# A two-layer transformer on one core: order of the first loads, the two norms between the layers, and halves at the end

## The chip, the core and the metric

The kernel runs on one core of a Trainium2 chip. The metric is device time in microseconds for one execution. Engines are called by their names in the profile: PE is TensorE (matrix products), PEld its weight loads, DVE is VectorE, ACT is ScalarE, POOL is GpSimd, SP is SyncE, which here only issues DMAs. Each engine works through its own instructions in the order in which the finished program has them, and waits on semaphores for the results of others.

## What is computed

The input x is 8×256 tokens of 128 numbers. Two layers follow, each an attention and a mixture of 8 experts of which every token takes 2, with a residual sum after each part:

```python
x = x + L0_attn(layernorm(x), ...)    # latent q/kv projections, rope, causal softmax
x = x + L0_ffn(layernorm(x), ...)
x = x + L1_attn(layernorm(x), ...)    # linear attention in segments of 32 tokens
x = x + L1_ffn(layernorm(x), ...)     # relu experts, not weighted
# L0_ffn, f being its input:
out = 0.5 * gelu(f @ shared_W + shared_b)
for e in range(8):
    out = out + combine[:, e:e+1] * (gelu(f @ W1[e] + b1[e]) @ W2[e] + b2[e])
out = (out - mean) * rsqrt(var + 1e-5) * gamma + beta
# L1_attn begins, x being its input (already a layernorm's output):
xn = x * rsqrt(mean(x * x) + 1e-6) * norm_w
q, k, v = xn @ Wq.T, xn @ Wk.T, xn @ Wv.T
```

So three norms follow one another between layer 0's experts and layer 1's projections: the norm of the experts' sum with gamma and beta, the layernorm of the new x (called `xl` in the kernel), and the root-mean-square norm of `xl`, whose factor r is applied after the projections.

## The kernel before

The tokens lie in 4 blocks of 512 (`NBLK`), each of 4 tiles of 128 tokens (`NT`); a block's x stays on chip as a tile [128, 4, 128]. Layer 0's attention (`attention0`) runs over rows of heads, two rows a block. Then each block goes through a chain of small steps and through the experts:

- `route0`: layernorm of x into `hrows`, transposes (L292), gate logits, choice of two experts, `dispatch`, which works out a slot for each token and copy, and eight indirect DMAs on POOL (L412) that scatter the rows `hrows` to the slots `xg` in DRAM.
- `experts`: 15 slots of 128 rows a block. SP loads the rows `xr` and the weights (256 KB a load), PE transposes the rows (L465, copied to `xrT` by DVE at L466) and does the products L482 and L494 with ACT's activation L489 between them; DVE copies the result `ys` (L502), SP stores it to `yg` in DRAM.
- `chosen`: eight indirect DMAs on POOL (L538) gather each token's two results as `yt`.
- `into_layer1` = `combine0` and `before1`. `combine0` adds the weighted `yt` to `acc` (eight operations of 128x128, L874), normalises `acc` by `layernorm` (scaled at L276), multiplies by gamma and adds beta on POOL (L883, L884), and adds the result to x on DVE (L886). `before1` takes the layernorm of x as `xl` (L276), then the statistics of `xl` for the second norm, transposes `xl` (L292) and projects it (L915).
- `attention1`: scores L1059, the mask product `at` on DVE (L1064), L1077, L1096 and further products on PE, with `vm` (L1002, L1140), `rec`, `on`, `xo` on POOL and DVE.
- `route1`, then `experts` and `chosen` again, and `finish`, which adds the two `yt` to x (L1281) and stores x to the output.

Every norm uses `moments` (per tile one statistics operation L265 and one aggregate L266 on DVE) and `rsqrt`: POOL adds eps (L256) and raises to the power −0.5 (L257), with the exponent from the tile `mhalf`.

At the start PE multiplies `wqa` by `wqb` and `wkva` by `wkvb` (L206, L208, with copies `oT` L207 and `wqkv` L211 to L214 on DVE), so that layer 0 has one projection; DVE multiplies the stacked layer-1 weights `wqkvu` by the norm's weight `nw` (L243). The loads are issued in text order on two queues: SP takes x0 to x3 first and then the weights, ACT takes `consts`, the rows of biases, and `nw`.

What is emitted when is set by `Lines`: a clock `now` that `go` advances by given times beside the attention's steps, and two queues, "chain" and "experts". Each step of a chain is due `APART` = 1.0 after the one before, or after the number that it yields; lags `SENT`, `STORED`, `BACK` = 5, 1, 5 stand before the experts, the gathers and `into_layer1` or `finish`. `behind(engine)` fixes what is emitted in it after the last instruction emitted for that engine; the rest is placed by the scheduler of the build. The result is one fixed order for each engine.

Of the kernel before, what the change touches and what calls it, by code (L numbers as in the profile page):

```python
# [34 lines left out]
ALU = mybir.AluOpType  # L35
# [28 lines left out]
    "before": P, "ones": P, "cap": E * NT, "upto": E * E, "slot": SL, "index": E,  # L64
    "ret": 2 * NSEG, "rev": E, "causal": P, "causalT": P, "pick": G * VA,
}
CAT, _n = {}, 0
for _k, _w in CONSTS.items():
    CAT[_k] = (_n, _n + _w)
    _n += _w  # L70
NCONST = _n


@with_exitstack
def two_layers(
# [67 lines left out]

    x_in = x.rearrange("(b t p) d -> b p t d", t=NT, p=P)
    out_v = out.rearrange("(b t p) d -> b p t d", t=NT, p=P)
    xs = []
    for b in range(NBLK):
        xb = tl(cp, [P, NT, D], f"x{b}")
        nc.sync.dma_start(out=xb, in_=x_in[b])
        xs.append(xb)  # L150

    def load(ap, shape, tag, eng=None):
        t = tl(cp, shape, tag)
        (eng or nc.sync).dma_start(out=t, in_=ap)
        return t
# [1 line left out]
    def load_row(ap, n, tag):  # L157
        return load(ap.partition_broadcast(P), [P, n], tag, nc.scalar)

    cs = load(consts, [P, NCONST], "consts", nc.scalar)  # L160

    def const(name):
        return cs[:, CAT[name][0] : CAT[name][1]]

    wqa_s = load(wqa, [D, QL], "wqa")
    wkva_s = load(wkva, [D, KVL], "wkva")
    wqb_s = load(wqb, [QL, D], "wqb")
    wkvb_s = load(wkvb, [KVL, KVH * HD * 2], "wkvb")
    wout_s = load(wout, [P, D], "wout")
    bout_s = load_row(bout, D, "bout")  # L170
    gw0 = load(gate_w0, [P, E], "gw0")
    shw = load(shared_w, [P, D], "shw")
    shb = load_row(shared_b, D, "shb")
# [21 lines left out]
    causb, causTb = tl(cp, [P, G, P], "causb", BF), tl(cp, [P, G, P], "causTb", BF)  # L195
    nc.vector.tensor_copy(causb, const("causal").unsqueeze(1).to_broadcast([P, G, P]))
    nc.vector.tensor_copy(causTb, const("causalT").unsqueeze(1).to_broadcast([P, G, P]))
    mhalf = tl(cp, [P, NT], "mhalf")
    nc.gpsimd.memset(mhalf, -0.5)


# [38 lines left out]
        yg.append(tl(dram, [SL * P, D], f"yg{h}"))  # L240


    nc.vector.tensor_scalar_mul(wqkvu[:, 0 : 3 * D], wqkvu[:, 0 : 3 * D], nw)  # L243


    vas = [tl(cp, [P, NT, H * VA + 32 - VA], f"va{k}") for k in range(2)]
    for t in vas:
# [4 lines left out]
    def rsqrt(src, eps):  # L252

        n = src.shape[1]
        r = tl(sm, [P, NT], "rsqrt")[:, 0:n]
        nc.gpsimd.tensor_scalar(r, src, eps, None, ALU.add)  # L256
        nc.gpsimd.tensor_tensor(r, r, mhalf[:, 0:n], ALU.pow)  # L257
        return r

# [570 lines left out]
    def route0(x, half):  # L830
        later = []
        xn = layernorm(x, half.rows, later)
        yield
        later[0]()
        yield
        with behind(PE):
            xT = transposed(xn, "xTf", "vec")
        yield
        lg = small("lg")
        with behind(PE):  # L840
            nc.vector.tensor_copy(lg, logits(xT, gw0))
            psh = bank().rearrange("p (t o) -> p t o", t=NT)
            for t in range(NT):
                nc.tensor.matmul(
                    psh[:, t, :], lhsT=xT[:, t * P : (t + 1) * P], rhs=shw, start=True, stop=True
                )
        half.acc = acc = tl(wk, [P, NT, D], "acc", bufs=NBLK)
        nc.vector.tensor_tensor(acc, psh, per_tile(shb), ALU.add)
        hots = half.hots
        m1, m2 = top2(lg, hots)  # L850
        yield 2 * APART
        yield from dispatch(half, b1s0)
        tot = small("tot", (P, NT))
        nc.vector.tensor_tensor(tot, m1, m2, ALU.add)
        nc.vector.reciprocal(tot, tot)
        gates = tl(wk, [P, 2, NT, E], "gates")
        for k, m in enumerate((m1, m2)):
            g = half.gates[:, k, :]
            nc.vector.tensor_tensor(g, m, tot, ALU.mult)
            nc.vector.tensor_tensor(gates[:, k], hots[:, k], last(g, E), ALU.mult)  # L860
        nc.vector.tensor_tensor(gates[:, 0], gates[:, 0], gates[:, 1], ALU.add)
        nc.scalar.activation(acc, acc, AF.Gelu)
        yield
        with behind(PE):
            nc.vector.scalar_tensor_tensor(
                acc, acc, 0.5, gated_bias(gates[:, 0], b2s0), ALU.mult, ALU.add
            )

    def combine0(x, half, yt):
# [6 lines left out]
                        acc[:, t, :], ALU.mult, ALU.add,  # L876
                    )
        yield
        later = []
        layernorm(acc, acc, later)  # L880
        yield
        later[0]()
        nc.gpsimd.tensor_tensor(acc, acc, per_tile(gam), ALU.mult)  # L883
        nc.gpsimd.tensor_tensor(acc, acc, per_tile(bet), ALU.add)  # L884
        yield
        nc.vector.tensor_tensor(x, x, acc, ALU.add)  # L886


    class Linear:
# [1 line left out]

    def before1(o, x):

        later = []
        xl = o.xl = layernorm(x, tl(wk, [P, NT, D], "xl"), later)
        yield
        later[0]()
        mv = moments(xl)
        ms = small("ms", (P, NT))
        nc.vector.tensor_tensor(ms, mv[:, :, 0], mv[:, :, 0], ALU.mult)  # L900
        nc.vector.tensor_tensor(ms, ms, mv[:, :, 1], ALU.add)
        r = rsqrt(ms, 1e-6)
        yield
        with behind(PE):
            xlT = transposed(xl, "xlT", "act", bufs=1)
# [278 lines left out]
    def route1(x, half):  # L1184
        later = []
        xn = layernorm(x, half.rows, later)
        yield
        later[0]()
        yield
        with behind(PE):  # L1190
# [79 lines left out]

    def into_layer1(b, half):
        yield from combine0(xs[b], half, half.yt)
        o = Linear()
        o.va = vas[b % 2]
        yield from before1(o, xs[b])
        linear[b] = o

    def finish(b, half):
        with behind(DVE):
            for k in range(2):  # L1280
                nc.vector.tensor_tensor(xs[b], xs[b], half.yt[:, k], ALU.add)  # L1281
        nc.sync.dma_start(out=out_v[b], in_=xs[b])
        yield

    def routed(b, layer):
# [119 lines left out]
```

## Time and profile before

| | us |
|---|---|
| median of 3 runs | 741.91 |
| the runs | 741.91, 733.67, 745.56 |
| profiled execution, its time | 770.52 |
| its span, first to last instruction | 768.8 |
| PE busy | 597.3 |
| PE idle, summed over its timeline | 154 up to its last product at 749.5 |
| mean granted clock of PE | 0.897 of full speed |

All lines of the profile are from the one profiled execution. A line of a timeline gives the start, the duration, the engine, the source line, the operation with output and inputs and the shape, and in brackets how long the engine stood idle before it and which instruction ended that wait. The chain of waits is followed back from the last instruction of the program. Between 0 and 20 us PE is busy 4.54 us: the first loads, `x0` at 6.1 and `wqa` at 10.84, come in; `nw` lands at 13.42 and `wvt`, part of `wqkvu`, at 15.55. PE's last product ends at 749.5; after it come the store of `yg`, the eight last gathers (752.93 to 762.6), the sums and the store of the output.

### The profile page before, as it was taken

Reading aid. Unit: us, or ns where it says so; the run is one execution under the profiler, and the core shown is the slowest. Engines: PE = TensorE matmul, PEld = TensorE weight load, DVE = VectorE, ACT = ScalarE, POOL = GpSimd, SP = SyncE. Lnnn points to the kernel's source line nnn. Section 1 sums busy time; section 2 is a strip of 40 time slices with the busy share of each in tenths; the row PEclk is TensorE's granted clock in tenths of the full one; section 3 lists DMA queues with packets and bytes.
Section 4 is the critical chain, followed back from the end, with each engine's and each line's share of the span. In section 5 each row is a group of like instructions: output and inputs, shape, how many; then the busy total and the mean of one; then the engine's idle time right before and its main releaser. Section 6 shows DMA issues by size and latency. Waiting matters only on the chain.

```text
span 768.8 us, 13323 instructions
## 1 busy us (share of the span) xinstructions
PE 597.3 (78%) x4654; PEld 454.3 (59%) x4654; DVE 402.1 (52%) x1161; ACT 339.3 (44%) x765; POOL 208.3 (27%) x269
## 2 busy tenths in 40 slices
PE   2578785998787788859988678879887799696880
PEld 1233343676464565439677567658685778595770
DVE  3656574446445565256845584656664476461111
ACT  0243332878758599415732231643234333342440
POOL 5200114010441304322123324050613250512303
PEclk9999978899989799878989796997988899897996
DMA  6500004353535133325434344354443456686761
GB/s 182 170 1 1 1 1 146 112 151 111 165 91 163 41 104 114 103 76 148 132 117 127 103 121 123 115 155 124 138 140 121 148 156 198 182 240 181 219 207 52
DMA packets 131890, 95.70 MB, mean 124 GB/s; under 512 B 8736, under 2 KB 114288, under 8 KB 131824
## 3 DMA queue, kind: packets, MB, share of 16 engines
q1 hardware_dynamic: 126400, 85.32, 37.7%
q0 software_dynamic: 4096, 8.40, 3.6%
q10 hardware_dynamic: 1328, 1.15, 0.5%
q8 instruction: 37, 0.61, 0.3%
q14 instruction: 29, 0.24, 0.1%
HBM read 77.79 MB, written 17.04 MB: 123 GB/s over the span
## 4 chain that ended last, share of the span: by engine, by line
PE 49%; DVE 16%; issue 9%; ACT 9%; DMA 7%; POOL 7%; SPq 2%; another core or an unknown queue 1%; POOLq 0%; ACTq 0%; DVEq 0%
PE mm L482 11%; PE mm L494 10%; PE sc L758 5%; POOL yt L538 3%; ACT at L705 2%; DMA w<-in_w 2%; PE mm L1077 2%; PE sc L763 2%; PE mm L1096 2%; DVE at L1064 2%; PE sc L915 2%; PE sc L1059 2%; PE mm L716 2%; DVE nmax L666 2%; ACT L489 1%
## 5 line engine op out<-in xcount | busy, mean ns | idle before, releaser
L489 ACT ACTIVATE hT<-mm,bias 128x128 f32<-128x128 f32 x480 | 135.9, 371 | 165.7 <-PE mm L482 123.4
L482 PE MATMUL mm<-xrT,w 128*128 128x128 f32 x960 | 149.7, 308 | 25.9 <-issue 10.6
L482 PEld LDWEIGHTS mm<-xrT,w 128*128 128x128 f32 x960 | 135.9, 219 | 42.1 <-issue 18.7
L494 PE MATMUL mm<-w,hT 128*128 128x128 f32 x960 | 144.2, 293 | 15.2 <-ACT hT L489 11.5
L494 PEld LDWEIGHTS mm<-w,hT 128*128 128x128 f32 x960 | 130.1, 206 | 22.8 <-ACT hT L489 18.3
L412 POOL DMA_INDIRECT xg<-hrows,slots x64 | 66.5, 1038 | 125.3 <-DVE slots L405 95.3
L538 POOL DMA_INDIRECT yt<-yg,slots x64 | 61.1, 955 | 87.1 <-DMA yg<-ys 52.9
L705 ACT ACTIVATE at<-sc 128x1024 f32<-128x1024 f32 x48 | 48.8, 1022 | 55.9 <-PE sc L763 32.8
L758 PE MATMUL sc<-qm,kxT 32*128 32x512 f32 x192 | 53.6, 679 | 14.6 <-DVE nmax L666 6.8
L758 PE MATMUL sc<-km,qT 32*128 32x512 f32 x192 | 53.6, 680 | 3.9 <-DVE qx L666 2.0
L502 DVE COPY ys<-mm 128x512 f32<-128x512 f32 (+1 forms) x32 | 21.0, 655 | 63.2 <-PE mm L494 47.7
L666 DVE TENSOR_REDUCE nmax<-sc 128x8 f32<-128x1024 f32 x32 | 38.8, 1219 | 25.3 <-PE sc L763 12.7
L1064 DVE TENSOR_TENSOR at<-sc,consts 128x1024 f32<-128x1024 f32 x32 | 38.0, 1215 | 17.2 <-PE sc L1059 6.6
L489 ACT ACT_TABLE_LOAD x27 | 34.6, 1283 | 11.0 <-PE mm L482 10.6
L256 POOL TENSOR_SCALAR rsqrt<-mv 128x4 f32<-128x4 f32 (+1 forms) x24 | 5.9, 245 | 102.2 <-DVE mv L266 96.9
L466 DVE COPY xrT<-mm 128x512 f32<-128x512 f32 (+1 forms) x32 | 20.8, 650 | 21.6 <-PE mm L465 21.1
L758 PEld LDWEIGHTS sc<-qm,kxT 32*128 32x128 f32 x192 | 14.4, 193 | 28.5 <-issue 10.2
L1083 ACT COPY rope<-mm 128x512 f32<-128x512 f32 x16 | 9.4, 586 | 49.0 <-PE mm L1077 27.8
L716 PE MATMUL mm<-at,vx 128*32 128x512 f32 x192 | 27.2, 635 | 4.7 <-ACT at L705 3.9
L666 DVE TENSOR_REDUCE qx<-sc 128x8 f32<-128x1024 f32 x16 | 19.6, 1224 | 20.2 <-PE sc L763 18.0
L1059 PE MATMUL sc<-pqm,kT 32*128 32x512 f32 x128 | 20.0, 696 | 12.8 <-DVE at L1064 9.0
L763 PEld LDWEIGHTS <-identb 128*128 128x128 bf16 x128 | 10.0, 98 | 33.6 <-issue 26.3
(211 smaller groups left out, 988.1 us busy)
## 6 DMA issues: line engine op xcount, KB each, us to landing
w<-in_w SPq DMA_DIRECT2D x240, 256.0 KB
xr<-xg SPq DMA_DIRECT2D x24, 256.0 KB
yg<-ys SPq DMA_DIRECT2D x24, 256.0 KB
xg<-zero SPq DMA_DIRECT2D x12, 256.0 KB
xr<-xg SPq DMA_DIRECT2D x8, 192.0 KB
yg<-ys SPq DMA_DIRECT2D x8, 192.0 KB
x<-in_x SPq DMA_DIRECT2D x4, 256.0 KB
xg<-hrows,slots POOLq DMA_INDIRECT x64
```

Source lines behind the costliest of these rows:

```text
L412: i = nc.gpsimd.indirect_dma_start(out=xg_h[:, :], out_offset=bass.IndirectOffsetOnAxis(ap=half.slots[:, k, t : t + 1], axis=0), in_=half. ...
L482: nc.tensor.matmul(ph[:, c * P : (c + 1) * P], lhsT=w1s[:, c * P : (c + 1) * P], rhs=xrT[:, t * P : (t + 1) * P], start=True, stop=True,)
L489: nc.scalar.activation(hT[:, c, :], src, func, bias=bias)
L494: nc.tensor.matmul(po[:, t * D : (t + 1) * D], lhsT=hT[:, c, :], rhs=w2s[:, c, :], start=(c == 0), stop=(c == NC - 1),)
L538: nc.gpsimd.indirect_dma_start(out=yt[:, k, t, :], out_offset=None, in_=yg[half.h][:, :], in_offset=bass.IndirectOffsetOnAxis(ap=half.slot ...
L666: return nc.vector.tensor_reduce(nm[:, js[0] : js[0] + 2, :], sc.rearrange("p j (i k) -> p j i k", i=G), AX.X, ALU.max, negate=True,)
L705: return nc.scalar.activation(pT[:, js[0] : js[0] + 2, :], sc, AF.Exp)
L716: nc.tensor.matmul(self.po[32 * j : 32 * j + 32, :], lhsT=self.vx[:, kt, j, :], rhs=self.pT_of[s][:, j, :], start=(kt == 0), stop=(kt == qt),)
L758: nc.tensor.matmul(out_, lhsT=lhsT, rhs=rhs, start=True, stop=mask is None)
L763: done[n].append(nc.tensor.matmul(out_.rearrange("p (i k) -> p i k", i=G), lhsT=identb, rhs=mask, start=False, stop=True,))
L1059: nc.tensor.matmul(sc[j].rearrange("p (i k) -> p i k", i=G), lhsT=pkT[rows, cols], rhs=pqm[rows, :, cols], start=True, stop=True,)
L1064: nc.vector.tensor_tensor(at[:, 2 * a : 2 * a + 2].rearrange("p j i k -> p (j i) k"), d.rearrange("p j (i k) -> p (j i) k", i=G), const("t ...
```

## The change

The first loads are issued in another order: x0, `wqa` and `wkva` on SP, `wqb` and `wkvb` on ACT's queue, `consts` in two pieces (the first 646 columns, then 990), and x1 to x3 behind them. The product of `wqkvu` and `nw` moves in the text from the set-up to the first `into_layer1`. `rsqrt` adds eps on DVE. `route0` adds beta to x on POOL once the layernorm's rows are scaled; the sum after the experts then leaves it out. `combine0` scales with gamma in the same operation as the mean's subtraction, before the power is known, and applies the power in the sum with x. `before1` takes both norms from one set of statistics of x: with v the variance of x, the mean of `xl` squared is v/(v+1e-5), so one power of 2×4 columns gives both factors. Steps that wait for a power are due 1.5 `APART` later. `finish` adds and stores in two halves of two tiles.

```diff
@@ -64,11 +64,12 @@
     "before": P, "ones": P, "cap": E * NT, "upto": E * E, "slot": SL, "index": E,
     "ret": 2 * NSEG, "rev": E, "causal": P, "causalT": P, "pick": G * VA,
 }
+SOON = ("cos", "sin", "sub", "first")
 CAT, _n = {}, 0
 for _k, _w in CONSTS.items():
     CAT[_k] = (_n, _n + _w)
     _n += _w
-NCONST = _n
+NCONST, NSOON = _n, CAT[SOON[-1]][1]
 
 
 @with_exitstack
@@ -143,12 +144,6 @@
 
     x_in = x.rearrange("(b t p) d -> b p t d", t=NT, p=P)
     out_v = out.rearrange("(b t p) d -> b p t d", t=NT, p=P)
-    xs = []
-    for b in range(NBLK):
-        xb = tl(cp, [P, NT, D], f"x{b}")
-        nc.sync.dma_start(out=xb, in_=x_in[b])
-        xs.append(xb)
-
     def load(ap, shape, tag, eng=None):
         t = tl(cp, shape, tag)
         (eng or nc.sync).dma_start(out=t, in_=ap)
@@ -157,17 +152,22 @@
     def load_row(ap, n, tag):
         return load(ap.partition_broadcast(P), [P, n], tag, nc.scalar)
 
-    cs = load(consts, [P, NCONST], "consts", nc.scalar)
+
+    xs = [load(x_in[0], [P, NT, D], "x0")]
+    wqa_s = load(wqa, [D, QL], "wqa")
+    wkva_s = load(wkva, [D, KVL], "wkva")
+    wqb_s = load(wqb, [QL, D], "wqb", nc.scalar)
+    wkvb_s = load(wkvb, [KVL, KVH * HD * 2], "wkvb", nc.scalar)
+    cs = tl(cp, [P, NCONST], "consts")
+    for cols in (slice(0, NSOON), slice(NSOON, NCONST)):
+        nc.scalar.dma_start(out=cs[:, cols], in_=consts[:, cols])
 
     def const(name):
         return cs[:, CAT[name][0] : CAT[name][1]]
 
-    wqa_s = load(wqa, [D, QL], "wqa")
-    wkva_s = load(wkva, [D, KVL], "wkva")
-    wqb_s = load(wqb, [QL, D], "wqb")
-    wkvb_s = load(wkvb, [KVL, KVH * HD * 2], "wkvb")
+    bout_s = load_row(bout, D, "bout")
+    xs += [load(x_in[b], [P, NT, D], f"x{b}") for b in range(1, NBLK)]
     wout_s = load(wout, [P, D], "wout")
-    bout_s = load_row(bout, D, "bout")
     gw0 = load(gate_w0, [P, E], "gw0")
     shw = load(shared_w, [P, D], "shw")
     shb = load_row(shared_b, D, "shb")
@@ -195,7 +195,7 @@
     causb, causTb = tl(cp, [P, G, P], "causb", BF), tl(cp, [P, G, P], "causTb", BF)
     nc.vector.tensor_copy(causb, const("causal").unsqueeze(1).to_broadcast([P, G, P]))
     nc.vector.tensor_copy(causTb, const("causalT").unsqueeze(1).to_broadcast([P, G, P]))
-    mhalf = tl(cp, [P, NT], "mhalf")
+    mhalf = tl(cp, [P, 2 * NT], "mhalf")
     nc.gpsimd.memset(mhalf, -0.5)
 
 
@@ -240,8 +240,6 @@
         yg.append(tl(dram, [SL * P, D], f"yg{h}"))
 
 
-    nc.vector.tensor_scalar_mul(wqkvu[:, 0 : 3 * D], wqkvu[:, 0 : 3 * D], nw)
-
 
     vas = [tl(cp, [P, NT, H * VA + 32 - VA], f"va{k}") for k in range(2)]
     for t in vas:
@@ -253,7 +251,7 @@
 
         n = src.shape[1]
         r = tl(sm, [P, NT], "rsqrt")[:, 0:n]
-        nc.gpsimd.tensor_scalar(r, src, eps, None, ALU.add)
+        nc.vector.tensor_scalar(r, src, eps, None, ALU.add)
         nc.gpsimd.tensor_tensor(r, r, mhalf[:, 0:n], ALU.pow)
         return r
 
@@ -830,8 +828,9 @@
     def route0(x, half):
         later = []
         xn = layernorm(x, half.rows, later)
-        yield
+        yield 1.5 * APART
         later[0]()
+        nc.gpsimd.tensor_tensor(x, x, per_tile(bet), ALU.add)
         yield
         with behind(PE):
             xT = transposed(xn, "xTf", "vec")
@@ -876,14 +875,20 @@
                         acc[:, t, :], ALU.mult, ALU.add,
                     )
         yield
-        later = []
-        layernorm(acc, acc, later)
-        yield
-        later[0]()
-        nc.gpsimd.tensor_tensor(acc, acc, per_tile(gam), ALU.mult)
-        nc.gpsimd.tensor_tensor(acc, acc, per_tile(bet), ALU.add)
-        yield
-        nc.vector.tensor_tensor(x, x, acc, ALU.add)
+
+        with behind(DVE):
+            mv = moments(acc)
+            r = rsqrt(mv[:, :, 1], 1e-5)
+            for t in range(NT):
+                nc.vector.scalar_tensor_tensor(
+                    acc[:, t, :], acc[:, t, :], mv[:, t, 0:1], gam, ALU.subtract, ALU.mult
+                )
+        yield 1.5 * APART
+        with behind(DVE):
+            for t in range(NT):
+                nc.vector.scalar_tensor_tensor(
+                    x[:, t, :], acc[:, t, :], r[:, t : t + 1], x[:, t, :], ALU.mult, ALU.add
+                )
 
 
     class Linear:
@@ -891,15 +896,25 @@
 
     def before1(o, x):
 
-        later = []
-        xl = o.xl = layernorm(x, tl(wk, [P, NT, D], "xl"), later)
-        yield
-        later[0]()
-        mv = moments(xl)
-        ms = small("ms", (P, NT))
-        nc.vector.tensor_tensor(ms, mv[:, :, 0], mv[:, :, 0], ALU.mult)
-        nc.vector.tensor_tensor(ms, ms, mv[:, :, 1], ALU.add)
-        r = rsqrt(ms, 1e-6)
+
+        xl = o.xl = tl(wk, [P, NT, D], "xl")
+        with behind(DVE):
+            mv = moments(x)
+            v, rr = mv[:, :, 1], small("norms", (P, 2, NT))
+            nc.vector.tensor_scalar(rr[:, 0], v, 1e-5, None, ALU.add)
+            nc.vector.reciprocal(rr[:, 1], rr[:, 0])
+            nc.vector.tensor_tensor(rr[:, 1], rr[:, 1], v, ALU.mult)
+            nc.vector.tensor_scalar(rr[:, 1], rr[:, 1], 1e-6, None, ALU.add)
+            rr = rr.rearrange("p a t -> p (a t)")
+            nc.gpsimd.tensor_tensor(rr, rr, mhalf, ALU.pow)
+        r = rr[:, NT:]
+        yield 1.5 * APART
+        with behind(DVE):
+            for t in range(NT):
+                nc.vector.tensor_scalar(
+                    xl[:, t, :], x[:, t, :], mv[:, t, 0:1], rr[:, t : t + 1],
+                    ALU.subtract, ALU.mult,
+                )
         yield
         with behind(PE):
             xlT = transposed(xl, "xlT", "act", bufs=1)
@@ -1184,7 +1199,7 @@
     def route1(x, half):
         later = []
         xn = layernorm(x, half.rows, later)
-        yield
+        yield 1.5 * APART
         later[0]()
         yield
         with behind(PE):
@@ -1270,16 +1285,21 @@
 
     def into_layer1(b, half):
         yield from combine0(xs[b], half, half.yt)
+        if b == 0:
+
+            nc.vector.tensor_scalar_mul(wqkvu[:, 0 : 3 * D], wqkvu[:, 0 : 3 * D], nw)
         o = Linear()
         o.va = vas[b % 2]
         yield from before1(o, xs[b])
         linear[b] = o
 
     def finish(b, half):
-        with behind(DVE):
-            for k in range(2):
-                nc.vector.tensor_tensor(xs[b], xs[b], half.yt[:, k], ALU.add)
-        nc.sync.dma_start(out=out_v[b], in_=xs[b])
+        for t in range(0, NT, 2):
+            x = xs[b][:, t : t + 2]
+            with behind(DVE):
+                for k in range(2):
+                    nc.vector.tensor_tensor(x, x, half.yt[:, k, t : t + 2], ALU.add)
+            nc.sync.dma_start(out=out_v[b][:, t : t + 2], in_=x)
         yield
 
     def routed(b, layer):
```

## The prediction

> **What bounds the kernel now.** I read the page's busy shares first, then its chain of waits, then TensorE's timeline for gaps, and last VectorE's and GpSimd's timelines inside the largest gaps. The page:
>
> ```profile
> PE 597.3 (78%) x4654; PEld 454.3 (59%) x4654; DVE 402.1 (52%) x1161; ACT 339.3 (44%) x765; POOL 208.3 (27%) x269
> ...
> PE 49%; DVE 16%; issue 9%; ACT 9%; DMA 7%; POOL 7%; SPq 2%; another core or an unknown queue 1%; POOLq 0%; ACTq 0%; DVEq 0%
> ```
>
> TensorE is busy for 78% of the span and is half of the chain; VectorE and GpSimd together are 23% of it. What the change can win is therefore the time in which TensorE stands and waits for them. Adding up the holes of TensorE's timeline gives 154 us, most of it in holes under 1.5 us that no part of this change addresses; two large ones sit at the chain it rewrites.
>
> ```profile
> 254.92 1.15 PE L292 MATMUL mm<-ident,xl 128*128 128x128 f32 x4 [7.59 <-DVE xl L276]
> 339.49 2.09 PE L1059 MATMUL sc<-pqm,kT 32*128 32x512 f32 x8 [6.71 <-DVE at L1064]
> ```
>
> Columns: start, duration, what, and in brackets the idle time before it with its releaser. The first is block 0's way from layer 0 to layer 1, followed back in the chain of waits:
>
> ```profile
> 247.17 1.13 DVE acc L276 x4
> 248.37 1.27 POOL acc L883
> 249.71 1.27 POOL acc L884
> ...
> 253.36 1.04 POOL rsqrt L257
> 254.92 1.15 PE mm L292 x4
> ```
>
> It is a serial relay VectorE–GpSimd–VectorE–GpSimd–VectorE. The second gap is block 1, in VectorE's timeline:
>
> ```profile
> 333.68 1.12 DVE L276 TENSOR_SCALAR acc<-acc,mv,rsqrt 128x128 f32<-128x128 f32 x4 [1.09 <-POOL rsqrt L257]
> 334.71 1.22 DVE L1064 TENSOR_TENSOR at<-sc,consts 128x1024 f32<-128x1024 f32 x1
> 337.51 0.69 DVE L886 TENSOR_TENSOR x<-x,acc 128x512 f32<-128x512 f32 x1 [1.59 <-POOL acc L884]
> 338.12 1.22 DVE L1064 TENSOR_TENSOR at<-sc,consts 128x1024 f32<-128x1024 f32 x1
> ```
>
> TensorE needs the two mask products L1064 of attention 1; they stand in VectorE's order behind the norm of `acc` and the sum L886, which wait for GpSimd. What blocks is the place in the order, not the work.
>
> **What the Trainium skill says.** "GPSIMD Engine Reference", section 4.1 Engine selection: two-input elementwise work belongs on VectorE, about twice as fast there. The trace agrees: 128x512 takes 1.27 us on GpSimd (L883) and 0.69 on VectorE (L886). "SBUF — State Buffer", section Who interferes with whom: a VectorE instruction with two SBUF inputs is blocked while a GpSimd instruction reads SBUF. The trace shows what looks like it: the 128x32 product L317 takes 1.27 us at 446.93, while L883 runs on GpSimd from 446.89. "TensorE: Matmul & The Clock Gate", its table of clock states: an idle window of some 3.4 us ends in half rate. The granted clock agrees in direction: 0.74 in the window 240–260 and 0.75 in 325–350, against 0.897 over the span.
>
> **The sum, part by part**, against the profiled execution (770.52 us, span 768.8). That one is 3.9% above the median of the runs, 741.91; I carry the ratio over.
>
> *First loads.* TensorE starts at 10.84 when `wqa` lands, but its work stops again until `xn` at 16.70; `xn` (16.30) waits in VectorE's order behind L243, the `wqkvu` product, which waits for the DMA of `wvt` until 15.57. The text moves L243 to the first chain, but in the changed program's instruction order it is still VectorE's 24th instruction, now between the two copies of `oT` (L207). So it stays at the start and holds the second copy. Its inputs: `nw` landed at 13.42 behind 11 ACT issues, and now stands behind 14, each about 0.4; the three `wq/wk/wv` loads have three issues fewer ahead on SP (0.37–0.39 each). I put the product at about 13.7, then the second `oT` copy, its matmul (0.68), three `wqkv` copies (0.5), `xn` at 15.6: −0.7. Bounds: −3 (loads as early as `x0`, which landed at 6.1) and +1.5 (the ACT queue slips by three waits).
>
> *Block 0's chain.* Gone: L883 and L884 (2×1.27), one add L256 (0.25), L886 (0.69) against four products of 128x128 (4×0.27), eight statistics of `xl`. New: four small VectorE operations (about 0.1–0.2 each) and a power of 128x8. A power of 128x2 takes 0.70 and of 128x4 1.04, so 1.72 by the same slope. That alone would be −2.5. But VectorE's new order puts `nmax` L666 (1.19), `qx` and the copy `os` L722 (0.68) between the two norms, which ran in the shadow of GpSimd before. Step by step from 244.4: scaling and eps 0.9, power 1.04, the four sums 1.1, statistics 1.0, the inserted 2.0, small operations 0.9, power 1.7, `xl` 0.4: about 253.9 for L292. −1.0; bounds 0 and −3.
>
> *Block 1's chain.* In the new order two L1064, `os`, `rec`, `on`, another L1064 and L746 all stand ahead of the statistics of `acc`. The eight sums L874 end at 330.94; two L1064 (1.13 each) to 333.2, `os` 0.6, L730 1.0, `rec` and `on` 0.5, two L565 with L567 and L570 2.5: L465 comes at about 338.0 instead of 347.01. Four L1059 (1.05) are then still to do, so −8.0. Late next is `xl`; by the same step lengths it is ready near 346.5, before TensorE reaches its transposes (near 348), so nothing is given back there. Bounds: −4 (`xl` or `xrT` L466, now behind the norm, holds TensorE) and −11 (the clock of that window rises from 0.75 to 0.897: 15.8 us of matmul become 13.2).
>
> *Blocks 2 and 3.* Two gaps at 448.54 (2.30) and 456.74 (1.99) and a stall of 0.64 come from L1064 and `cap` L382 behind norm work and the 1.27 block of L317. I take 3 of the 4.9. In block 3 VectorE waits 1.58 and 1.36 for GpSimd, with a TensorE gap of 2.07: −2. Bounds for both together: 0 and −8.5.
>
> *Route 1 of block 2.* Its power waited behind eight final gathers of block 0 (588.74–598.6) and TensorE then stood 4.57. In the new GpSimd order it stands ahead of them. Half: −2.3; bounds 0 and −4.6.
>
> *End.* The last gather lands at 764.23; then two sums (0.69 each) and a store. By halves: two sums of 128x256 (0.42 each) before the first store, two hidden under it, a second store of half the size: −0.6; bounds 0 and −1.
>
> *At nothing.* The early addition of `beta` to `x` (a 128x512 sum on GpSimd, 1.27 by L884, four times) runs while VectorE and TensorE do the routing; without that cover it costs up to 1.27 each, +5 in all. The eps additions moved to VectorE: 0.1 each, 24 times before, beside its 48% idle. Four more store issues on SP, 0.39 each, queued ahead of weight loads: hidden by the buffers of the weights; 1.6 without.
>
> Sum: −0.7 −1.0 −8.0 −3.0 −2.0 −2.3 −0.6 = −17.6, 752.9 us in that execution, a ratio of 0.977, **725 us** on the median. With all bounds at their good end (−3, −3, −11, −8.5, −4.6, −1 = −31) it is 712; with all at their poor end (+1.5, 0, −4, and nothing else) 739.5, or 741.0 with the 1.6 of the stores.
>
> **Rivals.** (a) *The gaps only move*, chance 0.27: block 1 gains half (−4), blocks 2 and 3 nothing, because the weights' loads and ACT hold TensorE there anyway; −7, **735 us**. For it: the idle shares of TensorE in many small holes, and ACT named for hidden-layer waits (L494, 11.5 us idle). Against: both large gaps name VectorE. (b) *GpSimd's order turns against it*, chance 0.10, slower: in the new order block 0's eight final gathers stand directly ahead of the eight scatters of block 2's layer 1, 16×1.25 = 20 us in one piece, and the gathers wait for the store of `yg` (a wait of that kind shows 4.94 at 312.65). If slots are ready when the gathers start, scatters are late by up to 4.9+10+1.8 (`vm`) = 16.7, at two places 33.4; with −15.3 left of the rest, +18, **759 us**. It decides from about 8 us per place on. Against: at 624.02 the scatters waited 3.82 for their slots, 25 us after the gathers ended. (c) *The change does not do what it says*: the product L243 is not moved, by the instruction order. That costs at most the 1.5 above and is inside the forecast.
>
> **How the numbers follow.** Forecast 0.63, rival (a) 0.27, rival (b) 0.10. The likeliest case's own range is 712–740; 8 in 10 with the run-to-run spread of before (733.67–745.56) and half of (a)'s poor end gives 710–743. About 2% (15 us) is what can be told from no change: 727 and below is faster. The forecast at 725 is near that border; its cases below it and a part above, with the block-1 clock gain on the other side, make faster 0.60, within 2% 0.30, slower 0.10.
>
> **What would show it.** Right: L292 after `xl` of block 0 about 1 us earlier with `nmax` and `os` in between; no gap of over 3 us ahead of L1059 in block 1 and L465 some 9 us earlier; a granted clock above 0.75 in that stretch; `xl` of block 1 ready before TensorE; no GpSimd wait of over 1 us in VectorE's norm chain of blocks 2 and 3. Wrong: a new gap of 4 us or more before the `xl` transposes of block 1 or the `xrT` copy, scatters L412 waiting on gathers, or VectorE's 24th instruction later than 15 us.

## The result and the profile after

| | before | after |
|---|---|---|
| median, us | 742.88 (733.67 to 747.98, 20 runs) | 736.45 (729.05 to 738.7, 20 runs) |
| ratio | | 0.9939, 95% interval 0.9911 to 0.9966 |
| profiled execution, us | 770.52 | 737.91 |

The change gains 0.6%, some 4.5 us: about a quarter of the 17.6 that the sum gave, and the forecast of more than 2% was wrong. The ratio compares, of each kernel, only the runs within 1.5% of its fastest; the quotient of the two medians is 0.991, and in the sets below the two measures differ by up to 0.007, so that smaller differences between kernels are not shown. The two profiled executions can't be subtracted: the one before lies 28 us above its median, the one after lies near its own. The kernel before took a median of 742.9, 779.4, 772.7, 772.9, 741.4 and 778.1 us in the six sets of comparisons of this study; only ratios go across. For the stages I set the profile after beside one of the old order with a like median (741.4 us in its set): the kernel with only the end by halves, `halves_only` below, whose orders are the old ones but for the final sums and stores. Its span is 739.8 us, the changed kernel's 736.1.

The page of the changed kernel, busy shares and chain of waits:

```profile
PE 583.3 (79%) x4654; PEld 443.2 (60%) x4654; DVE 408.8 (56%) x1177; ACT 341.9 (46%) x767; POOL 197.6 (27%) x233
...
PE 3%; DMA 2%; POOL 2%; issue 2%; ACT 0%; DVE 0%; POOLq 0%; SPq 0%; ACTq 0%; DVEq 0%
```

This chain could be followed back only through the last part of the span (its shares add up to 9%), so it says nothing of the stages before; the gaps of TensorE's timeline have to be read instead. First the old order, TensorE's timeline of `halves_only`, of which only lines with a gap that is spoken of below are shown (start, duration, what, idle time before it and its releaser):

```profile
256.98 1.15 PE L292 MATMUL mm<-ident,xl 128*128 128x128 f32 x4 [7.59 <-DVE xl L276]
342.96 2.09 PE L1059 MATMUL sc<-pqm,kT 32*128 32x512 f32 x8 [14.10 <-DVE at L1064]
410.03 1.49 PE L1059 MATMUL sc<-pqm,kT 32*128 32x512 f32 x8 [2.20 <-DVE vm L1140]
423.64 1.24 PE L292 MATMUL mm<-ident,hrows 128*128 128x128 f32 x4 [5.67 <-DVE hrows L276]
427.27 2.07 PE L482 MATMUL mm<-xrT,w 128*128 128x128 f32 x8 [2.39 <-DVE xrT L466]
446.13 1.14 PE L1059 MATMUL sc<-pqm,kT 32*128 32x512 f32 x8 [2.31 <-DVE at L1064]
580.70 1.63 PE L494 MATMUL mm<-w,hT 128*128 128x128 f32 x8 [4.58 <-ACT hT L489]
678.61 1.09 PE L465 MATMUL mm<-ident,xr 128*128 128x128 f32 x4 [4.68 <-DMA xr<-xg]
```

And, picked in the same way, the changed kernel's (its L290, L728, L1074, L463 and L480 are L292, L730, L1059, L465 and L482 of before):

```profile
258.59 1.24 PE L290 MATMUL mm<-ident,xl 128*128 128x128 f32 x4 [5.94 <-DVE xl L914]
339.92 1.92 PE L728 MATMUL mm<-consts,os 128*128 128x36 f32 x8 [6.86 <-DVE os L720]
402.85 2.08 PE L480 MATMUL mm<-xrT,w 128*128 128x128 f32 x8 [4.14 <-DVE on L1120]
426.18 2.09 PE L1074 MATMUL sc<-pqm,kT 32*128 32x512 f32 x8 [11.01 <-DVE rsqrt L254]
672.15 1.12 PE L463 MATMUL mm<-ident,xr 128*128 128x128 f32 x4 [8.28 <-DMA xr<-xg]
690.86 2.08 PE L480 MATMUL mm<-xrT,w 128*128 128x128 f32 x8 [6.42 <-DMA w<-in_w]
```

The gaps that the forecast promised to shorten did get shorter: block 0 from 7.59 to 5.94, block 1 from 14.10 to 6.86, and those at 446 and 581 are gone. But there is a gap of 11.01 that no part of the sum contained, one of 4.14, and longer waits for the last block's rows and weights. Up to its last product TensorE stands idle for 142.4 us in the old order (721.6 less 579.2 busy) and 134.6 in the new (717.9 less 583.3): 7.8 us less, though the four gaps that got shorter give back 15.8. Its busy time is 4.1 us longer, so its last product ends only 3.7 us earlier. Why the same number of products took longer stays open; the products right after a long gap did take about twice as long here (L1074 2.09 us at 426.18, behind the 11.01, and 1.14 at 414.03).

What the gap of 11 us waits for stands in VectorE's timeline of the changed kernel:

```profile
415.22 0.28 DVE L263 BATCH_NORM_STATS2 bnst<-x 128x6 f32<-128x128 f32 x1
415.54 0.18 DVE L264 BATCH_NORM_AGGREGATE mv<-bnst 128x2 f32<-128x6 f32 x1
423.42 0.29 DVE L263 BATCH_NORM_STATS2 bnst<-x 128x6 f32<-128x128 f32 x1 [7.71 <-POOL x L1164]
423.63 1.21 DVE L1079 TENSOR_TENSOR at<-sc,consts 128x1024 f32<-128x1024 f32 x1
...
426.02 0.68 DVE L464 COPY xrT<-mm 128x512 f32<-128x512 f32 x1
```

and in GpSimd's:

```profile
413.16 0.99 POOL L536 DMA_INDIRECT yt<-yg,slots  x1 [7.55 <-issue]
...
421.96 0.94 POOL L536 DMA_INDIRECT yt<-yg,slots  x1 [0.30 <-issue]
422.93 0.46 POOL L1164 TENSOR_TENSOR x<-x,hr 128x128 f32<-128x128 f32 x1
```

Block 0's attention 1 ends with four sums of the retrieved part into x (L1164, on GpSimd, 0.46 us). The last of them stands behind the eight gathers of block 2's experts, 413.16 to 422.90. The statistics of route 1 wait for it, and the masks L1079 of block 1, which TensorE needs next, stand behind these statistics in VectorE's order; so does the copy `xrT` for the next experts' products.

VectorE's wait for this sum is not new. The old order has it too, 8.59 us in `halves_only`, and TensorE did not stand through it:

```profile
410.92 0.68 DVE L466 COPY xrT<-mm 128x512 f32<-128x512 f32 x1
420.19 0.29 DVE L265 BATCH_NORM_STATS2 bnst<-x 128x6 f32<-128x128 f32 x1 [8.59 <-POOL x L1149]
```

```profile
411.65 3.21 PE L482 MATMUL mm<-xrT,w 128*128 128x128 f32 x16
```

There the copy `xrT` stands ahead of the waiting statistics, so TensorE has experts' products from 411.65 to 417.98 and is left with gaps of 5.67 and 2.39. In the new order masks and copy both stand behind the wait, and TensorE has nothing to do. What the change made is this re-laying, not the wait: in five profiles of kernels that have the old order here (`before`, `before_again`, `loads_only`, `before_last`, `halves_only`) VectorE waits 7.68 to 8.59 us for the sum, in five with the new one (the changed kernel, `after_again`, `chain_only`, `all_held`, `all_last`) 7.68 to 7.71. The gap of 4.14 at 402.85 lies at another place of this kind, a sum L1164 behind the eight scatters L410, for which VectorE waits 5.69.

The start, VectorE of the changed kernel:

```profile
14.66 0.42 DVE L1290 TENSOR_SCALAR wqkvu<-wqkvu,nw 128x384 f32<-128x384 f32 x1 [3.54 <-DMA nw<-in_norm_w]
14.99 0.27 DVE L207 COPY oT<-mm 32x128 f32<-32x128 f32 x1
...
16.45 2.44 DVE L274 TENSOR_SCALAR xn<-x,mv,rsqrt 128x128 f32<-128x128 f32 x6
```

`wqa` now lands in time for TensorE to start at 4.12 instead of 10.84, but the product with `nw` waits until 14.66 and holds the second copy of `oT`; `xn` comes at 16.45, against 16.30 before.

### The profile page after: what moved, and what is told of

It reads as the page before. It is cut to its first block, busy times and chain, and to the rows that moved or that the text cites. A ratio compares the mean times of both kernels' runs of the same rounds, so it can differ in the third digit from the quotient of the medians.

```text
span 736.1 us, 13320 instructions
## 1 busy us (share of the span) xinstructions
PE 583.3 (79%) x4654; PEld 443.2 (60%) x4654; DVE 408.8 (56%) x1177; ACT 341.9 (46%) x767; POOL 197.6 (27%) x233
## 5 line engine op out<-in xcount | busy, mean ns | idle before, releaser
L480 PE MATMUL mm<-xrT,w 128*128 128x128 f32 x960 | 146.3, 303 | 22.3 <-DMA w<-in_w 10.0
L480 PEld LDWEIGHTS mm<-xrT,w 128*128 128x128 f32 x960 | 132.8, 215 | 38.2 <-DVE xrT L464 10.2
L492 PE MATMUL mm<-w,hT 128*128 128x128 f32 x960 | 139.5, 287 | 7.9 <-ACT hT L487 6.6
L492 PEld LDWEIGHTS mm<-w,hT 128*128 128x128 f32 x960 | 126.1, 201 | 15.4 <-ACT hT L487 13.3
L410 POOL DMA_INDIRECT xg<-hrows,slots x64 | 66.5, 1039 | 127.9 <-DVE slots L403 104.6
L756 PE MATMUL sc<-km,qT 32*128 32x512 f32 x192 | 55.4, 711 | 3.2 <-DVE qx L664 1.7
L255 POOL TENSOR_TENSOR rsqrt<-rsqrt,mhalf 128x4 f32<-128x4 f32 (+1 forms) x20 | 18.7, 939 | 105.2 <-DVE rsqrt L254 60.1
L1079 DVE TENSOR_TENSOR at<-sc,consts 128x1024 f32<-128x1024 f32 x32 | 37.9, 1217 | 6.9 <-PE sc L1074 6.9
L463 PE MATMUL mm<-ident,xr 128*128 128x128 f32 x120 | 21.8, 308 | 14.0 <-DMA xr<-xg 13.1
L1074 PE MATMUL sc<-pqm,kT 32*128 32x512 f32 x128 | 20.9, 727 | 13.1 <-DVE rsqrt L254 11.0
```

The costliest lines, as they stand in the source:

```text
L410: i = nc.gpsimd.indirect_dma_start(out=xg_h[:, :], out_offset=bass.IndirectOffsetOnAxis(ap=half.slots[:, k, t : t + 1], axis=0), in_=half. ...
L463: nc.tensor.transpose(pt[:, t * P : (t + 1) * P], xr[:, t, :], ident)
L480: nc.tensor.matmul(ph[:, c * P : (c + 1) * P], lhsT=w1s[:, c * P : (c + 1) * P], rhs=xrT[:, t * P : (t + 1) * P], start=True, stop=True,)
L492: nc.tensor.matmul(po[:, t * D : (t + 1) * D], lhsT=hT[:, c, :], rhs=w2s[:, c, :], start=(c == 0), stop=(c == NC - 1),)
L756: nc.tensor.matmul(out_, lhsT=lhsT, rhs=rhs, start=True, stop=mask is None)
L1079: nc.vector.tensor_tensor(at[:, 2 * a : 2 * a + 2].rearrange("p j i k -> p (j i) k"), d.rearrange("p j (i k) -> p (j i) k", i=G), const("t ...
```

## The experiments

Each set ran beside the kernel before; ratios are to that kernel.

**The first profile again, and the change in parts.** `loads_only` is the diff's part on the loads (with the move of the `wqkvu` product), `chain_only` its part on the chain (`rsqrt`, `route0`, `combine0`, `before1`, `route1`). `chain_only` has the order of the full change on TensorE and GpSimd, `loads_only` the old one. `all_held` is the full change with

```diff
         if b == 0:
-            nc.vector.tensor_scalar_mul(wqkvu[:, 0 : 3 * D], wqkvu[:, 0 : 3 * D], nw)
+            with behind(DVE):
+                nc.vector.tensor_scalar_mul(wqkvu[:, 0 : 3 * D], wqkvu[:, 0 : 3 * D], nw)
```

> The kernel before, unchanged: a second profile, because the first one took 770.52 us against a median of 742. If the stages decide (theory), its TensorE gaps of 7.59 us at block 0's xl transposes and 6.71 us ahead of block 1's L1059 come back within 1 us, and the 28 us that it lacks come from many places; if the first profile's gaps were an accident of that execution (rival), at least one of the two is under 3 us.

> The kernel before with the new order of the first loads alone (the order of TensorE and GpSimd is the old one throughout). Theory: TensorE gets wqa near 4 us, but the wqkvu product still stands between the two oT copies and waits for nw until about 14.7, so the time changes by -0.5 to +1.5 us, ratio 0.999 to 1.002. Rival: the changed profile only shows an unlucky landing of nw, and the loads give what they were worth at most, -3 us.

> The kernel before with the changed chain alone (power, beta, eps on VectorE, later due times), old loads, old end; TensorE's and GpSimd's orders are those of the full change. Theory: this part carries all of the full change, ratio 0.990 to 0.997, with the 11 us gap ahead of L1074 in block 2 there again. Rival: the chain gives nothing (1.000) and the full change's 0.6% comes from loads and halves.

> The full change with the wqkvu product really held to the first chain (placed behind VectorE's last instruction there); every other instruction keeps its place on every engine. Theory: nw no longer holds the second oT copy, so TensorE's first projection comes 3 to 4 us earlier than the 18.03 of the changed kernel, and 2 to 4 us of it reach the end: ratio to the kernel before 0.989 to 0.991. Rival: the start's gain is absorbed by the waits for scatters and weights later on, ratio 0.994 as the change has it.

Measured: `before_again` shows gaps of 7.58 and 6.69 us at the two places, so they belong to the order and not to one execution. `loads_only` 1.0004 (0.9969 to 1.0040): nothing. `chain_only` 0.9910 (0.9877 to 0.9944): the chain alone gives what the full change gives, and loads and end add nothing that these intervals show. In its profile, block 1's gap of 6.69 has no successor above 1.4 us, and the new gap is there, 11.02. `all_held` 0.9900 (0.9870 to 0.9930): TensorE's first projection comes at 16.1 instead of 18.0, less than the 3 to 4 expected, since the copies of `oT` still stand behind the statistics of x1; and it makes no difference to the end that these intervals could show. Its ratio lies in the theory's range, but `chain_only`, with the old loads, has nearly the same in the same set, so neither theory nor rival is shown.

**The new gap: first by its sum.** `all_hr` moves L1164 to VectorE in the full change, `before_hr` does so in the old kernel, `all_eps` puts the addition of eps back on GpSimd.

```diff
-            nc.gpsimd.tensor_tensor(x[:, t, :], x[:, t, :], hr, ALU.add)
+            nc.vector.tensor_tensor(x[:, t, :], x[:, t, :], hr, ALU.add)
```

> The full change, unchanged, beside the next three on one chip. Theory: the ratio of 0.9939 was the whole of it, so 0.988 to 0.997 again, with the 11.0 us gap ahead of block 1's L1074, at which VectorE's statistics wait for GpSimd's sum L1164 behind eight gathers. Rival: the gap belongs to one execution; then it is under 6 us here.

> The full change with the sum of the retrieved part (L1164, 16 times 128x128) on VectorE instead of GpSimd. Theory: the 11.0 us gap is the price of that sum's place behind eight gathers in GpSimd's order; without it L1074 starts within 2 us of the work before it, and 6 to 11 us reach the end: ratio to the kernel before 0.980 to 0.987. Rival: the masks L1079 then wait for something else (the power of route 1, also behind those gathers), or VectorE's 16 additional sums (0.28 to 0.46 each) take their place: ratio within 0.003 of the full change.

> The kernel before with the same sum on VectorE; TensorE's order is unchanged. Theory: in the old order TensorE waits there for hrows, whose power stands behind the gathers anyway, so nothing is gained: 0.997 to 1.002. Rival: the sum behind the gathers costs the old kernel as much, and its ratio falls to 0.99 or below, so that the change didn't make this wait.

> The full change with eps added on GpSimd again (23 small operations of about 0.24 us move back). Theory: the place of eps costs nothing by itself; within 0.004 of the full change either way, which includes a few places where the scheduler lays TensorE's order otherwise. Rival: the addition on VectorE, in order behind other work, is what holds L1074 (the trace names it as the releaser), and the time falls by 5 us or more.

Measured: `after_again` 0.9975 (0.9938 to 1.0012), just outside the range of 0.988 to 0.997 and with an interval that takes in 1, with the gap at 11.00; `all_hr` 0.9984 (0.9945 to 1.0024); `before_hr` 1.0050 (1.0015 to 1.0085), slower than either expectation, though its median, 771.2 us, is not above the 772.7 of the kernel before, so a loss is not shown; `all_eps` 0.9959 (0.9908 to 1.0010), its gap 10.52, now ahead of L480, which waits for `xrT`. So the place of eps costs nothing that these intervals show, and taking the sum away from GpSimd doesn't help. TensorE's timeline of `all_hr` says why:

```profile
429.51 2.08 PE L480 MATMUL mm<-xrT,w 128*128 128x128 f32 x8 [1.93 <-DVE rsqrt L254]
438.58 0.48 PE L290 MATMUL mm<-ident,hrows 128*128 128x128 f32 x1 [7.00 <-DVE hrows L274]
```

The 11 us became 1.93 and 7.00: the power of route 1 stands behind the same eight gathers, as the rival said. My first theory, that it was the sum alone, fell; sum and power both stand behind the gathers.

**Then by the gathers.** `all_g4` emits these gathers four steps later, so that sums and power of block 0 come first on GpSimd. This is not an edit of one place: the build lays other orders anew too, and in the profiles TensorE's differs from that of the full change from the product at 426.18 on. `all_last` does the same for block 1's last gathers against block 3's route 1, `before_last` that in the old kernel, and `all_both` combines both with a delay for block 0's last gathers and the held `wqkvu` product.

```diff
-        lines.add("chain", steps(), STORED, use)
+        lines.add("chain", steps(), STORED + (4 if (b, layer) == (2, 0) else 0), use)
```

(`all_last` and `before_last` have `(1, 1)` in place of `(2, 0)`; `all_both` has 4 for `(2, 0)`, `(0, 1)` and `(1, 1)`.)

> The full change with the eight gathers of block 2's experts (layer 0) emitted four steps later, so that block 0's sums of the retrieved part and the power of its route 1 stand ahead of them in GpSimd's order. Theory: the 11.0 us gap ahead of L1074 was TensorE waiting out these gathers; now no gap above 3 us is left between the end of block 0's attention 1 and its hrows, and 5 to 11 us of it reach the end: ratio to the kernel before 0.980 to 0.990. Rival: the stall only moves to what waits for the late gathers (block 2's xl), and the ratio stays within 0.003 of the full change's.

> The full change with the eight last gathers of block 1 (needed for its output alone) emitted four steps later, behind the sums and the power of block 3's route 1; TensorE's order is the same. Theory: the last block's chain is on the path that sets the end, its sums stood 8 us behind these gathers (VectorE idle 7.94 at 659), and what the change gained earlier ran into this: hrows of the last block comes 7 to 9 us earlier, TensorE's wait of 7.1 us for xr shrinks, ratio to the kernel before 0.982 to 0.990. Rival: TensorE's other work, not the chain, sets the end there; then the time is that of the full change within 0.003.

> The kernel before with block 1's last gathers behind block 3's sums and power in the same way. Theory: this place held the last block in the old order as well, so the old kernel gains as much, ratio 0.988 to 0.995; then the change neither made nor removed this limit, it only ran into it. Rival: the old kernel still had other work there, and nothing is gained: 0.997 or above.

> The full change with both delays, block 0's last gathers delayed by four steps too, and the wqkvu product held to the first chain. Theory: the two gains add, ratio to the kernel before 0.970 to 0.982, the fastest of all. Rival: the waits for weights and the lower clock give most of it back, no better than the better of the two alone.

Measured: `all_g4` 0.9734 (0.9652 to 0.9817), more than expected; `all_last` 0.9966 (0.9936 to 0.9996), that of the full change, with the same order on TensorE; `before_last` 1.0039 (1.0009 to 1.0070), no gain, as its rival said; `all_both` 0.9815 (0.9738 to 0.9893), inside the theory's range but not better than `all_g4`, which is what its rival said. Where `all_last` lost its gain shows in VectorE's timeline and TensorE's, in this order:

```profile
651.51 0.86 DVE L274 TENSOR_SCALAR hrows<-x,mv,rsqrt 128x128 f32<-128x128 f32 x3
```

```profile
667.02 0.64 PE L290 MATMUL mm<-ident,hrows 128*128 128x128 f32 x4
```

The last block's `hrows` are ready at 652.4, some 12 us earlier than in `after_again` (664.3), but TensorE comes to their transposes only at 667.0 (669.3 there), because the fixed order puts experts' products ahead of them. My theory, that the chain sets the end at this place, fell.

**Is it the delay alone?** The full change and the old kernel with the same delay, the chain alone with it, and the halves alone:

> The kernel before with block 2's eight gathers behind block 0's sums and the power of route 1, as in the run with the full change that gained most. Theory: the old order had 5.0 and 2.4 us of gaps at these gathers, so it gains less: ratio 0.990 to 0.998, and the chain's own gain shows as the difference to the full change with the same delay. Rival: it gains as much (0.970 to 0.980); then the delay is the whole of that result and the change is worth nothing even without its new wait.

> The full change with block 2's gathers delayed, once more, since the first result rests on 6 runs. Theory: 0.968 to 0.982 again. Rival: the first was a lucky set, and the ratio is 0.985 or above.

> The changed chain alone (old loads, old end) with block 2's gathers delayed; TensorE's and GpSimd's orders are those of the full change with the delay. Theory: the chain is all of it, ratio within 0.004 of the full change with the delay. Rival: loads and halves carry part once the wait is gone, and this one is slower by 0.006 or more.

> The kernel before with the end by halves alone. Theory: from the landing of the last gather to the end of the span it saves 0.3 to 1 us of some 4.5, and the additional store issues cost nothing: 0.997 to 1.001. Rival: the four additional store issues stand ahead of weight loads on SP and cost up to 1.6 us or more: 1.002 or above.

| | without the delay | with it |
|---|---|---|
| kernel before | 1 | 0.9896 (0.9862 to 0.9931) |
| full change | 0.9939 (0.9911 to 0.9966), 0.9975 (0.9938 to 1.0012) | 0.9777 (0.9731 to 0.9823), 0.9734 (0.9652 to 0.9817) |
| chain alone | 0.9910 (0.9877 to 0.9944) | 0.9819 (0.9770 to 0.9867) |
| halves alone | 0.9969 (0.9942 to 0.9997) | |

The delay gives the old kernel 1.0%, slightly more than expected. With the delay in both, the change is worth 0.9777/0.9896 = 0.988, 1.2%; without it 0.3 to 0.6% by the ratios. That would mean that the gathers' place took part of the change's gain away, but it is not shown: by the medians it is 0.989 with the delay in both and 0.991 without. The ratio near 0.977 isn't the forecast come true after all either, for about half of it belongs to the delay. `all_g4_again` came out as expected; `chain_g4`, 0.004 above it, lies on the border between its theory and its rival. TensorE's timeline of `all_g4_again` at the place of the 11 us:

```profile
418.62 3.16 PE L480 MATMUL mm<-xrT,w 128*128 128x128 f32 x16 [2.21 <-DVE xrT L464]
421.57 1.61 PE L492 MATMUL mm<-w,hT 128*128 128x128 f32 x8
423.03 0.60 PE L290 MATMUL mm<-ident,hrows 128*128 128x128 f32 x4
```

2.21 us is left: the sum now runs at 416.63 and the power at 418.77, ahead of the gathers, which start at 420.01. So the delay takes the wait away at this place. What it gains in time is not shown to be that wait: from the changed kernel's profile to this one TensorE's idle time falls by 0.9 us only (134.6 to 133.7), its busy time by 8.8 (583.3 to 574.5), for a reason that stays open. Further on the same pattern appears again, in VectorE's timeline of this kernel, where block 1's last gathers run from 614.07 to 623.87 on GpSimd:

```profile
624.39 0.35 DVE L1133 SCALAR_TENSOR_TENSOR x<-xo,sm,x 128x128 f32<-128x128 f32 x1 [13.53 <-POOL x L1164]
```

TensorE stands 15.53 us there. The last two kernels remove this as well: `g4_last` delays both sets of gathers by four steps, `g4_last_hr` has the sums on VectorE besides.

> The full change with block 2's gathers delayed and block 1's last gathers behind block 3's sums and power as well; TensorE's order is that of the delay alone up to two products. Theory: with the first wait gone, TensorE meets the same kind of wait at block 1's last gathers (15.5 us ahead of L480 at 626 in all_g4_again, VectorE's x waiting 13.5 for GpSimd's L1164); removing that too gives 0.958 to 0.972. Rival: TensorE waits there for the loads of weights or rows instead, as at the last block, and the ratio stays 0.973 to 0.982.

> As g4_last, with the sums of the retrieved part on VectorE instead of GpSimd, so that no scatter or gather stands ahead of any of them. Theory: the remaining 4 us at block 0's scatters goes too, 0.003 to 0.008 below g4_last. Rival: 16 more sums on VectorE (0.28 to 0.46 each) cost what they save, within 0.003 of g4_last or above it.

Measured: `g4_last` 0.9700 (0.9626 to 0.9774), in its theory's range; `g4_last_hr` 0.9805 (0.9727 to 0.9883), not below it, as the rival said. The gap of 15.53 is gone in `g4_last`, whose largest gaps in this part are 5.19 (`xTf`) and 5.10 us (no releaser shown). It has the lowest ratio of the study, but its interval overlaps those of `all_g4`, so a gain from closing that gap is not shown; the rival's reading, that the gap returns as other waits, isn't excluded. One large gap stands in `g4_last` that nothing here explains, 9.41 us at 404.30, ahead of a product that waits for VectorE's `vm`; `chain_only`, `after_again` and `all_last` have it too (9.32 to 9.42), the profile of the full change only 1.53. Both beat the two kernels of this case.

## Why the prediction was wrong

By its own steps, with `halves_only` as the old order and the changed kernel's profile:

| step | forecast, us | found, us |
|---|---|---|
| first loads | −0.7 | +0.15 (`xn` 16.45 against 16.30) |
| block 0's chain | −1.0 | −1.65 (gap 7.59 to 5.94) |
| block 1's chain | −8.0 | −7.2 (gap 14.10 to 6.86), though L463 comes only 4.1 us earlier |
| blocks 2 and 3 | −5.0 | −2.3 at 446; the rest not separable |
| route 1 of block 2 | −2.3 | −4.6 (the gap of 4.58 is gone) |
| end | −0.6 | −1.1 (last sum to end of span, 4.47 to 3.36, from the profile of the kernel before; `halves_only` has this part already, 3.44) |
| waits at GpSimd's blocks, 400 to 430 | not in the sum | +4.9 (2.20+5.67+2.39 became 4.14+11.01) |
| last block's rows and weights | not in the sum | +5.5 (4.68 for rows, 2.17 and 2.32 for weights became 8.28+6.42) |

**The step that failed is the sum itself**: it took off the gaps that it named and put new waits in the orders re-laid behind block 1's chain at nothing, with a poor end of "+1.5, 0, −4, and nothing else". In the profiles TensorE's order is the old one up to block 1's chain and another from the products L492 at 331.24 on, and the new orders of VectorE and GpSimd were read only at a few places. In its place the runs showed new waits: 11.01 and 4.14 us where 5.67, 2.39 and 2.20 had been, and 8.28 and 6.42 at the last block where 4.68, 2.17 and 2.32 had been. The gaps that closed add up to 15.6 us without the end (1.65+7.24+2.31+4.58 less 0.15), the new waits to 10.4, so −5.2; the measured idle time fell by 7.8 with 4.1 more of busy time, the last product came 3.7 earlier, and the ratio says −4.5. The list is not complete: a gap of 5.55 at 645.20 of the old order became 2.24, and one of 3.57 at 532.53 has no counterpart. The balance is worked out from two executions and holds to a few microseconds only.

A reading behind the sum was wrong too: that most of TensorE's 154 us of idle time lay in holes under 1.5 us, out of the change's reach. In that profile these holes hold about 65 us, less than half; the longer ones, in which new waits can come and go, hold the rest.

That VectorE stands at the eight gathers in this gap is shown by runs: away with the delay (to 2.21), moved to the power with `all_hr`, there, 11.00 to 11.02, in all five profiles of the new order without the delay, a moved sum or a moved eps. That TensorE stands with it, where in the old order it did not, is read from the orders of the two timelines; no run put the copy `xrT` back ahead of the statistics alone. How much of the missing 13 us this gap accounts for is not shown, since the delay also re-laid TensorE's order. That the longer waits at the last block are the price of arriving there earlier was not shown; `all_last` tells only that an earlier chain does not help, since TensorE's order holds it.

Block 0's step was right in its mechanism, if low by 0.65 us in size: `nmax` and `os` run between the two norms, at 253.69 and 254.89, and the power of 128x8 took 1.64 us (1.72 by the slope). VectorE's timeline of the changed kernel:

```profile
251.64 1.14 DVE L889 SCALAR_TENSOR_TENSOR x<-acc,rsqrt,x 128x128 f32<-128x128 f32 x4 [0.68 <-POOL rsqrt L255]
...
253.69 1.20 DVE L664 TENSOR_REDUCE nmax<-sc 128x8 f32<-128x1024 f32 x1
...
254.89 0.66 DVE L720 COPY os<-mm 128x512 f32<-128x512 f32 x1
...
258.19 1.12 DVE L914 TENSOR_SCALAR xl<-x,mv,norms 128x128 f32<-128x128 f32 x4 [1.75 <-POOL norms L909]
```

Block 1's was near in the size of the gap and half right in its mechanism. The masks no longer wait for the norm, but in this pair of profiles the eight sums of `yt` end at 337.0 (334.42 in `halves_only`), not 330.94: they waited for the gathers' landing, and a gap of 6.86 is left where "no gap of over 3 us" was to be seen. L463 comes at 346.43 against 350.48, 4.1 us earlier and not 9, and the granted clock in 325 to 350 is 0.73, not above 0.75. In `chain_only`, in a set where the kernel before took 779 us and with TensorE busy for 599.7 us instead of 583.3, the largest gap there is 1.32.

"At nothing" held, as far as these intervals show, for eps (`all_eps`, `after_again`) and for the four more stores (`halves_only` is not slower). For `beta` it is open: in the changed profile its sum L833 (97.04 to 98.30) stands on GpSimd ahead of a power, and TensorE's gap behind it is 3.54 against 2.79 us in `halves_only`; no run isolates it. The reading that the `wqkvu` product stays at the start was right; it cost no more than the bounds, but its loads came no earlier, so the start gave nothing (`loads_only`).

Rival (a), that gaps only move, came nearest, with 735 us for a median of 736.45, but by another way: block 1's gap lost 7.2 us where (a) had 4, other gaps closed too, and new orders of VectorE and TensorE at waits for GpSimd took most of it. That its number came out is in part luck. Rival (b) named the right resource, gathers standing ahead on GpSimd, and the wrong customer: it priced the scatters, and what waited were the sums and the power of the block one layer further. The scatters at 585.42 waited 14.98 us, for their slots and not for gathers. The trace before held the warning, and the prediction does not mention it: its gap of 4.91 ahead of `hrows` was already a wait at these gathers, and VectorE stood there for 7.80 us:

```profile
428.00 1.24 PE L292 MATMUL mm<-ident,hrows 128*128 128x128 f32 x4 [4.91 <-DVE hrows L276]
```

```profile
424.55 0.29 DVE L265 BATCH_NORM_STATS2 bnst<-x 128x6 f32<-128x128 f32 x1 [7.80 <-issue]
```

"SBUF — State Buffer" of the Trainium skill (Who interferes with whom) was cited for a shared read path; no run here separates its effect.

## What to carry to other kernels

When a change makes a planner lay out fixed orders anew, the gaps that it closes are only one side of the sum: list the new order of each engine that carries long blocks, here eight gathers of 1.25 us each on GpSimd, and for each short operation behind such a block ask who waits for it and what is queued behind that waiter. Look also at waits that are already there: in the old order TensorE had products to do while VectorE waited, in the new one it had none, and a wait of the same length on VectorE cost TensorE more. Moving the short operation to another engine didn't help here, because the next one on its chain stood behind the block too; moving the block took both waits away, but laid other orders anew with it, so a gain that comes with such a move is not yet the gain of the wait. And a chain that was made faster gained nothing here where the consumer's own fixed order came to it later.

## What the runs showed that I had not expected

The kernel before took medians from 741.4 to 779.4 us in six sets, 5% apart, while within a set they spread by 2 to 3%, and a ratio of one and the same change came out as 0.9939 and 0.9975 (0.991 and 0.992 by medians). The sets with 741.4 and 778.1 ran on a chip of the same number, so the chip isn't shown to be the reason. Gaps move with it: block 1's was 14.10 us where the kernel before took 741 and 6.69 us in `before_again`, where it took 779. A gap read from one profile is therefore known to its mechanism, not to its size.
